# A second buffer for the padded C tile of a Mamba-2 mixer's B/C chains

## The chip, the cores and the metric

The kernel runs on one core of one Trainium2 chip. A core has a matrix engine with its weight loader (PE and PEld in the profile), a vector engine (DVE), a scalar engine for activations and copies (ACT), GpSimd (POOL) and a sync engine (SP) that issues most of the DMAs. The metric is the device time of one execution in microseconds; lower is better.

## The reference

The input x has 4 batches of 256 tokens and 512 channels, all float32. A layer norm gives xn, which feeds two branches:

- a Mamba-2 mixer: `in_proj` gives a gate and x (8192 channels each), B and C (8 groups of 128 channels each) and dt (128 heads). x, B and C pass a causal convolution of 4 taps along the tokens and a silu. Per head, scores C·B with decays multiply x·dt within chunks and between them; the result is gated, normalised by group and projected by `out_proj` to 512 channels.
- a ternary FFN (1792 wide): `silu(x·gate) * (x·up)`, times `down`, then a silu.

The output is `x + mixer * ffn`. What the change touches is the convolution of C:

```python
conv = conv_general_dilated(transpose(xBC, (0, 2, 1)), conv_w, (1,), [(K - 1, 0)],
                            feature_group_count=CONV_DIM, ...)
xBC = silu(transpose(conv + conv_b[None, :, None], (0, 2, 1)))
B = xBC[..., DIN:DIN + G * N].reshape(b, l, G, N)
C = xBC[..., DIN + G * N:].reshape(b, l, G, N)
```

## The kernel before

There are two stages. The first, `front` (L193), lasts until about 302 us; in it the FFN runs on PE while smaller pieces of the mixer are set between its products. The second (from L789) goes over the 64 column tiles of the mixer's x, with the output projection between them.

**The FFN of the front** is a loop of 28 steps (L561): two halves of the tokens by 14 tiles of the FFN's width. A step multiplies by the gate weights (`project_exact`, L289, tile pg), takes a silu on ACT (L566, sg), multiplies by the up weights (L289, pu), combines both on DVE (L575), copies the result on ACT as hh (L583), takes the remainder on DVE as hl (L587), and two steps later multiplies both by the down weights (L297). The integer weights come by DMA on SP (L221) and are cast on POOL (L229).

**The pieces** are called three times in each step (`next(pieces)`); one call is a turn. `all_pieces` (L498) starts a chain `bc_pieces(g)` for group g every 8 turns, from turn 11 on. A new chain is put ahead of the older one, so in a turn that both have, the new one's instructions come first on every queue. Chain g does, a turn to a line:

- turns 0 to 3: four products of two matmul halves each, by Strassen's scheme over B and C at once, in one PSUM bank px; after each, ACT copies the bank into a half of a padded tile (L432): cpad, cpad, then xpad, xpad. cpad holds C and xpad holds B, with three zero columns ahead of each batch of 256 tokens. The next product adds into the same bank, so it waits for the copy.
- turns 4 and 5: three more products (pz and pq); DVE adds them to the halves (L442, L445, L448).
- turn 6: on ACT the last tap of C into cT and of B into bT (L178); on DVE two more taps of C (L182)
- turn 7: the last tap of C and one of B on DVE
- turns 8 and 10: the silus (L187); turns 8 and 9: two more taps of B
- from turn 11: three rounds of scores of C by B on PE (L469, pg); DVE masks two of them (L472) and ACT copies the third (L474) into sc, which SP stores (L476).

Turn 8 of chain g is turn 0 of chain g + 1: the new chain's first copy into cpad stands on ACT's queue ahead of the old chain's silu of C. It writes what the old chain's taps of C read, the last of them issued on DVE in the turn before. In the source the tile cpad, like bT, cT, sc and xpad, has one buffer.

Other pieces share the queues: the sums for the next chain's Strassen weights (L143 to L147, from w, loaded on SP at L134), the dt path, and decay scans of the first ten column tiles (L190, tile em: loaded at L494, stored at L489).

**The order** of the instructions on an engine is that of the source within each stage (`manual_schedule`, L597 and L789). Where the two stages meet, a planner at build time interleaves them on a queue: the load of gm from the second stage (L790) stands among the front's DMAs on SP at 103.9 us, and the first load of a row tile (L622) at 299.3 us.

**PSUM and SBUF.** FFN products, pz, pq and score products take turns in the three banks of `ps_proj`. The tiles of the front's pools (pre, one_of, fp, f2, hp, ep, one behind the other) are laid over again by those of the second stage; a tile there waits for the tiles of the front that lie under it.

Of the kernel before, what the change touches and what calls it, by code (L numbers as in the profile page):

```python
# [43 lines left out]
F32 = mybir.dt.float32  # L44
# [6 lines left out]
P = 128  # L51
NB = 4
# [11 lines left out]
TAPS = 4  # L64
PADW = L + TAPS - 1
# [16 lines left out]
def mixer_ffn(ctx: ExitStack, tc: tile.TileContext, x, in_w, conv_w, conv_b, dt_bias, a_log, d_col,  # L82
              norm_w, out_w, gate_t, up_t, down_t, gate_s, up_s, down_s, out):
    nc = tc.nc
# [46 lines left out]
    def load_w(*tiles):  # L131
        w = wp.tile([P, 2, KT, P], F32, name="w")
        for n, i in enumerate(tiles):
            nc.sync.dma_start(w[:, n], in_w[i])  # L134
        return w

    def blocks(w):
        return [w[:, n, k:k + 2, :] for n in (0, 1) for k in (0, 2)]

    def combine_to(s1, s2, s4, s3, w):  # L140

        a11, a12, a21, a22 = blocks(w)
        nc.vector.tensor_add(s1, a21, a22)  # L143
        nc.vector.tensor_sub(s2, s1, a11)
        yield
        nc.vector.tensor_sub(s4, a12, s2)
        nc.vector.tensor_sub(s3, a11, a21)  # L147
        yield

    def factors(w, s):  # L150
        a11, a12, a21, a22 = blocks(w)
        return a11, a12, a22, s[:, 0], s[:, 1], s[:, 2], a21
# [10 lines left out]
    def halves(xpad):  # L163
        return [xpad[:, 2 * h:2 * h + 2, TAPS - 1:] for h in range(2)]
# [3 lines left out]
    def by_batch(v):  # L168
        return v.rearrange("p (b l) -> p b l", l=L)

    def product(pp, a, b, start, ks=range(KT // 2)):

        for k in ks:
            nc.tensor.matmul(pp, a[:, k, :], b[:, k, :], start=start and k == 0,  # L174
                             stop=k == KT // 2 - 1, skip_group_check=not start)

    def last_tap(i, xT, xpad):
        nc.scalar.mul(xT, xpad[:, :, TAPS - 1:], cw[:, i, TAPS - 1:TAPS])  # L178

    def conv_taps(i, xT, xpad, taps=range(TAPS - 1)):  # L180
        for k in taps:
            nc.vector.scalar_tensor_tensor(xT, xpad[:, :, k:k + L], cw[:, i, k:k + 1], xT,  # L182
                                           ALU.mult, ALU.add)

    def conv_silu(i, xT):
        xf = xT.rearrange("p b l -> p (b l)")
        nc.scalar.activation(xf, xf, AF.Silu, bias=cb[:, i:i + 1])  # L187
# [5 lines left out]
    def front(pre, one_of, fp, f2, hp, ep):  # L193
# [6 lines left out]
        nc.gpsimd.affine_select(out=upto, in_=ones, compare_op=ALU.is_ge, fill=0.0, base=0,  # L200
                                pattern=[[1, P]], channel_multiplier=-1)
        upto_b = upto.unsqueeze(1).to_broadcast([P, NB, P])
        cpad = one_of.tile([P, NB, PADW], F32, name="cpad")
        nc.gpsimd.memset(cpad[:, :, 0:TAPS - 1], 0.0)
        bT, cT = [one_of.tile([P, NB, L], F32, name=n) for n in ("bT", "cT")]
        sc = one_of.tile([P, ROW], F32, name="sc")
        wdt = one_of.tile([P, KT, P], F32, name="wdt")
# [213 lines left out]
        def bc_pieces(g):  # L421


            i_b, i_c = CT + g, CT + G + g
            bpad_h, cpad_h = halves(xpad), halves(cpad)
            a11, a12, a22, s1, s2, s4, s3 = held.pop("a")
            w = load_w(2 * CT + G + g + 1, 2 * CT + g + 1) if g + 1 < G else load_w(0, CT)
            px = ps_t.tile([P, HALF], F32, name="px", tag="t")
            for a, b, to in ((a11, x11, cpad_h[0]), (s2, t2, cpad_h[1]), (s3, t3, bpad_h[1]),
                             (a22, t4, bpad_h[0])):  # L430
                product(px, a, b, a is a11)
                nc.scalar.copy(to, by_batch(px))  # L432
                if a is s2:
                    s = scp.tile([P, 3, KT // 2, P], F32, name="s")
                    held["a"] = factors(w, s)
                    sums = combine_to(s[:, 0], s[:, 1], s[:, 2], blocks(w)[2], w)
                if a is s3 or a is a22:
                    next(sums)
                yield
            pz = ps_proj.tile([P, HALF], F32, name="pz", tag="proj")  # L440
            product(pz, a12, x21, True)
            nc.vector.tensor_add(cpad_h[0], cpad_h[0], by_batch(pz))  # L442
            pq = ps_proj.tile([P, HALF], F32, name="pq", tag="proj")
            product(pq, s1, t1, True)
            nc.vector.tensor_add(bpad_h[1], bpad_h[1], by_batch(pq))  # L445
            yield
            product(pq, s4, x22, False)
            nc.vector.tensor_add(cpad_h[1], cpad_h[1], by_batch(pq))  # L448
            yield
            last_tap(i_c, cT, cpad)  # L450
            last_tap(i_b, bT, xpad)
            conv_taps(i_c, cT, cpad, (0, 1))
            yield
            conv_taps(i_c, cT, cpad, (2,))
            conv_taps(i_b, bT, xpad, (0,))
            yield
            conv_silu(i_c, cT)
            conv_taps(i_b, bT, xpad, (1,))
            yield
            conv_taps(i_b, bT, xpad, (2,))  # L460
            yield
            conv_silu(i_b, bT)
            for _ in range(1 if g + 1 < G else 3):
                yield
            diag = sc[:, 0:T].rearrange("p (b c i) -> p b c i", c=NC, i=P)
            for kb, qb in ((0, 0), (1, 1), (0, 1)):
                pg = ps_proj.tile([P, NB, P], F32, name="pg", tag="proj")
                for b in range(NB):
                    nc.tensor.matmul(pg[:, b, :], bT[:, b, kb * P:(kb + 1) * P],  # L469
                                     cT[:, b, qb * P:(qb + 1) * P], start=True, stop=True)  # L470
                if kb == qb:
                    nc.vector.tensor_tensor(diag[:, :, kb, :], pg, upto_b, ALU.mult)  # L472
                else:
                    nc.scalar.copy(sc[:, T:], pg.rearrange("p b i -> p (b i)"))  # L474
                yield
            nc.sync.dma_start(scores[g], sc)  # L476
# [21 lines left out]
        def all_pieces():  # L498

            turn, chains = 0, [first_pieces()]  # L500
            later = []
            while chains or later or turn < 11 + 8 * G:
                if turn == 6:
                    later.append(dt_pieces())
                if turn >= 11 and (turn - 11) % 8 == 0 and (turn - 11) // 8 < G:
                    chains.insert(0, bc_pieces((turn - 11) // 8))
                if turn == 24:
                    later.append(early_pieces(turn))
                if turn > 11 and (turn - 11) % 8 == 4 and len(chains) > 1:
                    chains.append(chains.pop(0))  # L510
                chains = [c for c in chains if next(c, chains) is None]
                later = [c for c in later if next(c, later) is None]
                turn += 1
                yield
# [82 lines left out]
    with (tc.manual_schedule(), tc.tile_pool(name="pre", bufs=NT) as pre,  # L597
          tc.tile_pool(name="one_of", bufs=1) as one_of, tc.tile_pool(name="fp", bufs=3) as fp,
          tc.tile_pool(name="f2", bufs=2) as f2, tc.tile_pool(name="hp", bufs=1) as hp,
          tc.tile_pool(name="ep", bufs=3) as ep):  # L600
        a, w = front(pre, one_of, fp, f2, hp, ep)
# [187 lines left out]
    with tc.manual_schedule():  # L789
# [4 lines left out]
        for i in range(CT):  # L794
            r, g = i % PER_G, i // PER_G
# [261 lines left out]
        for b in range(NB):  # L1057
            a, f, xb = whole[b]
# [75 lines left out]
```

## Time and profile before

| | us |
|---|---|
| median of three runs | 1728.27 (1727.25 to 1728.54) |
| the profiled execution's own time | 1728.53 |
| its span | 1726.8 |
| the front with the edited chains, about | 43 to 302 |

| engine | busy, us | share of the span |
|---|---|---|
| PE | 1713.8 | 99% |
| PEld | 1107.0 | 64% |
| DVE | 1449.1 | 84% |
| ACT | 1069.9 | 62% |
| POOL | 215.2 | 12% |

In the profile a group of instructions is named by its source line, its engine and `out<-in`, the tiles that it writes and reads. A timeline row gives the start and the duration in us, the engine, the line, the operation, and in brackets the idle time of that engine just before with what ended it. A row of the waits names who waited for whom, the total in us, how often, and the longest. The span is that of the instructions; the execution's own time is 1.73 us longer.

### The profile page before, as it was taken

The page shows a single profiled execution, that of the slowest core. Times are in us where ns is not written, and L with a number is a line of the kernel's source. Part 1 is how long each engine was busy: PE and PEld are TensorE (multiplying, and loading weights), DVE is VectorE, ACT ScalarE, POOL GpSimd, SP SyncE. Part 2 cuts the span into 40 slices and gives each one's busy share as a digit, 9 for nine tenths or more (in the row PEclk, how much of TensorE's full clock was granted, in tenths as well). Part 3 has the DMA queues.
Part 4 walks back from the last instruction along what each step waited for, and adds up shares of the span by engine and source line. Part 5 has one row for each costly group of instructions (what it writes and reads, how often), then busy time and mean ns, then how long its engine had stood idle before and what let it go on. Part 6 is the DMA issues. An engine that isn't in the chain of part 4 may idle for free.

```text
span 1726.8 us, 22575 instructions
## 1 busy us (share of the span) xinstructions
PE 1713.8 (99%) x8494; PEld 1107.0 (64%) x8494; DVE 1449.1 (84%) x1742; ACT 1069.9 (62%) x1428; POOL 215.2 (12%) x238
## 2 busy tenths in 40 slices
PE   8999999999999999999999999999999999999999
PEld 6666667555566666666666666666666666666687
DVE  5768787788888898889888988898889888898876
ACT  4544333688766666666666666666666666666640
POOL 3222323000000000111011100110111011101110
PEclk9999999999999999999999999999999999999999
DMA  6357666576766675777677767776776676767775
GB/s 226 91 168 243 210 230 200 209 222 206 236 198 206 195 216 170 202 201 207 177 206 200 214 188 210 205 216 193 210 203 200 185 210 198 201 172 211 210 229 169
DMA packets 161931, 347.27 MB, mean 201 GB/s; under 512 B 15136, under 2 KB 52896, under 8 KB 161824
## 3 DMA queue, kind: packets, MB, share of 16 engines
q1 hardware_dynamic: 139136, 292.89, 49.4%
q0 software_dynamic: 22688, 52.96, 17.4%
q8 instruction: 67, 1.10, 0.3%
q14 instruction: 40, 0.33, 0.1%
HBM read 236.48 MB, written 81.00 MB: 184 GB/s over the span
## 4 chain that ended last, share of the span: by engine, by line
PE 94%; DVE 3%; DMA 1%; ACT 1%; issue 0%; SPq 0%; ACTq 0%; DVEq 0%
PE px L174 28%; PE po L749 22%; PE pq L174 14%; PE py L693 10%; PE pz L174 7%; PE pp L289 5%; PE tp L649 3%; PE pf L297 2%; PE pg L469 1%; DVE cT L182 1%; PE pv L711 1%; DMA sqacc<-sq 1%; DMA ya<-gated 0%; PE pd L322 0%; DMA wd_i<-in_down_t 0%
## 5 line engine op out<-in xcount | busy, mean ns | idle before, releaser
L174 PE MATMUL px<-xc,w 128*128 128x512 f32 x576 | 271.8, 594 | 0.0
L182 DVE SCALAR_TENSOR_TENSOR xT<-xpad,cw,xT 128x1024 f32<-128x1024 f32 x192 | 246.1, 1282 | 10.0 <-ACT xT L178 5.7
L190 DVE TENSOR_TENSOR_SCAN m<-m,after 128x1024 f32<-128x1024 f32 x108 | 246.5, 2282 | 0.0
L749 PE MATMUL po<-wo,ya 128*128 128x256 f32 x768 | 176.5, 379 | 0.0
L643 DVE TENSOR_TENSOR m<-m,gm 128x1024 f32<-128x1024 f32 x128 | 150.7, 1219 | 14.9 <-ACT m L635 14.9
L693 PE MATMUL py<-m,v 128*64 128x128 f32 x2048 | 160.7, 276 | 0.0
L962 POOL DMA_DIRECT2D sqacc<-sq x54 | 46.1, 853 | 877.4 <-ACT sq L881 812.5
L749 PEld LDWEIGHTS po<-wo,ya 128*128 128x128 f32 x768 | 141.5, 190 | 17.0 <-issue 0.2
L174 PE MATMUL pz<-xnT,w 128*128 128x512 f32 x288 | 145.8, 592 | 0.0
L174 PEld LDWEIGHTS px<-xc,w 128*128 128x128 f32 x576 | 99.4, 190 | 72.2 <-issue 68.9
L174 PE MATMUL px<-xnT,w 128*128 128x512 f32 x288 | 141.8, 615 | 0.0
L174 PE MATMUL px<-xc,s 128*128 128x512 f32 x288 | 135.7, 594 | 2.2 <-ACT cpad L432 2.1
L174 PE MATMUL pq<-xnT,s 128*128 128x512 f32 x288 | 136.2, 595 | 0.2 <-DVE xpad L913 0.2
L174 PE MATMUL pq<-xc,s 128*128 128x512 f32 x288 | 135.3, 592 | 0.0
L635 ACT ACTIVATE m<-m 128x1024 f32<-128x1024 f32 x128 | 134.3, 1058 | 0.6
L649 PEld LDWEIGHTS tp<-ident,xT 128*128 128x128 f32 x512 | 67.8, 141 | 99.5 <-issue 86.4
L693 PEld LDWEIGHTS py<-m,v 128*64 128x64 f32 x2048 | 117.7, 137 | 20.3 <-issue 19.1
L749 PE MATMUL po<-tw,sy 128*128 128x256 f32 x512 | 115.9, 379 | 0.0
L749 PEld LDWEIGHTS po<-tw,sy 128*128 128x128 f32 x512 | 97.2, 190 | 13.2
L855 ACT COPY gT<-px 128x512 f32<-128x512 f32 x64 | 37.5, 586 | 107.8 <-PE px L174 105.0
L693 PE MATMUL py<-mo,v 128*64 128x128 f32 x1024 | 99.7, 273 | 0.0
L174 PEld LDWEIGHTS pq<-xc,s 128*128 128x128 f32 x288 | 54.7, 190 | 68.9 <-issue 62.2
(182 smaller groups left out, 3116.4 us busy)
## 6 DMA issues: line engine op xcount, KB each, us to landing
m<-rows SPq DMA_DIRECT2D x108, 512.0 KB, 6.5
w<-in_in_w SPq DMA_DIRECT2D x144, 256.0 KB, 6.9
mo<-rows SPq DMA_DIRECT2D x128, 256.0 KB, 7.3
gated<-yg SPq DMA_DIRECT2D x64, 512.0 KB, 8.4
ya<-gated SPq DMA_DIRECT2D x30, 1024.0 KB, 7.2
sqacc<-sq POOLq DMA_DIRECT2D x54, 512.0 KB, 6.2
wo<-in_out_w SPq DMA_DIRECT2D x64, 256.0 KB, 6.9
acc<-sa POOLq DMA_DIRECT2D x23, 512.0 KB, 6.0
```

Source lines behind the costliest of these rows:

```text
L174: nc.tensor.matmul(pp, a[:, k, :], b[:, k, :], start=start and k == 0, stop=k == KT // 2 - 1, skip_group_check=not start)
L182: nc.vector.scalar_tensor_tensor(xT, xpad[:, :, k:k + L], cw[:, i, k:k + 1], xT, ALU.mult, ALU.add)
L190: nc.vector.tensor_tensor_scan(m, m, after, 0.0, ALU.add, ALU.mult)
L289: nc.tensor.matmul(pp, w[:, k * P:(k + 1) * P], part[:, k, :], start=(k == 0 and part is xh), stop=(k == KT - 1 and part is xl))
L297: nc.tensor.matmul(pf, part[:, i * P:(i + 1) * P], wd, start=(f == 0 and part is hh), stop=(f == FT - 1 and part is hl))
L635: nc.scalar.activation(m, m, AF.Exp)
L643: nc.vector.tensor_mul(m, m, gm[:, 0:T])
L649: nc.tensor.transpose(tp[:, b, :], xT[:, b, c * P:(c + 1) * P], ident)
L693: nc.tensor.matmul(py[d, q * P:(q + 1) * P], v[:, b, h, :], m, start=False, stop=True, skip_group_check=True)
L749: nc.tensor.matmul(po, a[:, k, :], b[:, k, :], start=start and k == 0, stop=k == HG - 1, skip_group_check=not start)
L855: nc.scalar.copy(gT[:, HALF:], px)
L962: nc.gpsimd.dma_start(sqacc, sq, accum_op=ALU.add)
```

## The change

The single tile cpad becomes two tiles of the same shape, cpad0 and cpad1, each with its zero columns written once by POOL. Chain g uses the one numbered g modulo 2. The rest of the chain, its products, copies, taps and their order, is as before; xpad keeps its one buffer.

```diff
-        cpad = one_of.tile([P, NB, PADW], F32, name="cpad")
-        nc.gpsimd.memset(cpad[:, :, 0:TAPS - 1], 0.0)
+        cpads = [one_of.tile([P, NB, PADW], F32, name=f"cpad{n}") for n in range(2)]
+        for cpad in cpads:
+            nc.gpsimd.memset(cpad[:, :, 0:TAPS - 1], 0.0)
...
             i_b, i_c = CT + g, CT + G + g
+            cpad = cpads[g % 2]
             bpad_h, cpad_h = halves(xpad), halves(cpad)
```

The tile takes 4,144 bytes in each partition.

## The prediction

> **What bounds the kernel now.** I read the page first, for the engine that is never idle.
>
> ```profile
> span 1726.8 us, 22575 instructions
> ...
> PE 1713.8 (99%) x8494; PEld 1107.0 (64%) x8494; DVE 1449.1 (84%) x1742; ACT 1069.9 (62%) x1428; POOL 215.2 (12%) x238
> ...
> PEclk9999999999999999999999999999999999999999
> ```
>
> PE is idle for 13 us in all, and its clock is granted in full. An edit that leaves PE's own work alone can hardly give more than those 13 us. The edited chains run only from 43 to 302 us, so I asked for the busy time of that stage, and then for its waits.
>
> ```profile
> 43.00:302.00 259.00, 256.79 (x1022) 175.83 (x1021) 199.33 (x210) 109.57 (x148) 73.33 (x69) 1.00 0.57 190
> ```
>
> Of 259.00 us PE is busy 256.79, the weight loader 175.83 and DVE 199.33: PE is the bound here too, DVE at 77% is not. The waits (us in total, times, longest):
>
> ```profile
> DVE cpad L448 <- PE pq L174: 18.2, 7, 3.8
> ...
> ACT cpad L432 <- DVE cT L182: 13.1, 5, 4.4
> ...
> PEld px L174 <- ACT cpad L432: 3.9, 4, 1.8
> ```
>
> The second line is the wait the edit removes: ACT's copy of a new chain's product into cpad waits for DVE's taps of the chain before. ACT loses 13.1 us there, but the end of the program is set by PE, and PE loses less: four waits of the weight loader, and it spends about 0.24 us between loads anyway, so 3.9 - 4 x 0.24 = 2.9 us. The PE timeline places them:
>
> ```profile
> 72.59 0.40 PE L297 MATMUL pf<-wd,hl 128*128 128x512 f32 x1
> 73.10 1.98 PE L174 MATMUL px<-xc,s 128*128 128x512 f32 x4
> ...
> 134.08 0.40 PE L289 MATMUL pp<-xl,wg 128*128 128x512 f32 x1
> 135.86 1.98 PE L174 MATMUL px<-xc,s 128*128 128x512 f32 x4 [1.38 <-ACT cpad L432]
> ...
> 165.16 0.40 PE L297 MATMUL pf<-wd,hl 128*128 128x512 f32 x1
> 165.99 1.98 PE L174 MATMUL px<-xc,s 128*128 128x512 f32 x4 [0.44 <-ACT cpad L432]
> ...
> 224.76 0.40 PE L289 MATMUL pp<-xl,wg 128*128 128x512 f32 x1
> 225.41 1.55 PE L174 MATMUL px<-xc,s 128*128 128x512 f32 x3 [0.25 <-ACT cpad L432]
> ```
>
> Neighbouring FFN matmuls start 0.23 us apart, so the products could have started at 72.82, 134.31, 165.39 and 224.99: stalls of 0.28, 1.55, 0.60 and 0.42 us, 2.85 us together, in chains 1, 3, 4 and 6. Chains 2, 5 and 7 pay nothing (chain 7's product starts at 254.95, 0.23 after 254.72).
>
> **The change part by part.**
>
> *Removed: the copy's wait on the taps.* The copy (0.59 us) still needs the first product and whatever stands ahead of it on ACT's queue.
>
> ```profile
> 133.69 0.62 ACT L583 CAST hh<-sg 128x512 fp32r<-128x512 f32 x1 [2.29 <-DVE sg L575]
> 135.22 0.59 ACT L432 COPY cpad<-px 128x512 f32<-128x512 f32 x1 [0.91 <-DVE cT L182]
> 135.70 1.15 ACT L187 ACTIVATE cT<-cT,cb 128x1024 f32<-128x1024 f32 x1
> ```
>
> Chain 1: product done 71.13, copy done by 71.76, ahead of 72.82; the whole 0.28 goes. Chain 4: product done 163.70, copy done 164.33, ahead of 165.39; 0.60 goes. Chain 6: the cast of hh ends 223.72, copy done 224.35, ahead of 224.99; 0.42 goes. Chain 3 differs: the cast ahead of the copy itself waited for DVE until 133.69 and ends 134.31, so the copy ends 134.94 and the product starts 134.99. Of 1.55, 0.87 goes. After a stall the second matmul also comes 0.53 us after the first instead of 0.43 (73.10 to 73.63); 0.10 more goes in chains 1, 4 and 6. Gross: 0.38 + 0.87 + 0.70 + 0.52 = 2.47 us.
>
> *What is late next.* ACT runs straight into L187, which waits for the same third tap; ACT gains only the 0.5 us by which that silu starts earlier. Behind it stand the sigmoid-gate and hh instructions and the next copy. In chain 4, hh waits for DVE until 167.14 and ends 167.75, so the next copy ends 168.38; the product that needs it could start at 169.67 - 0.70 = 168.97, so PE does not see it. Next is the B tile xpad, which keeps one buffer: its copy needs the third B tap, done at 140.38 in chain 3, while its product, done 141.41 before, comes at 140.54. It holds by 0.16.
>
> *Does DVE follow?* Yes, mostly: the first line of the waits says that in seven chains of eight DVE stands idle for PE before L448, 18.2 us in all, so its backlog ends once per chain and an earlier PE starts the next taps earlier. The exception is chain 4:
>
> ```profile
> 171.95 0.42 DVE L143 TENSOR_TENSOR s<-w 128x256 f32<-128x256 f32 x1 [1.32 <-DMA w<-in_in_w]
> 180.51 0.67 DVE L472 TENSOR_TENSOR sc<-pg,upto 128x512 f32<-128x512 f32 x1
> ```
>
> From 171.95 DVE is busy to 181.18, and PE's gate product at 181.63 takes over the bank that L472 empties: 0.45 us of room. That stretch starts with a weight load which SP issued at 164.76 behind a store that waits for a scan on DVE; both move with the gains of chains 1 and 3 (1.25), not with that of chain 4. PE can get ahead of them by 0.45 less 0.05 for the hand-over, 0.40, so 0.30 of chain 4's 0.70 is given back. Net: 2.47 - 0.30 = 2.17 us.
>
> *Added: one memset* (0.11 us, L204). POOL is idle for 3.01 us until 6.72 behind it, waiting for a weight load, so it costs nothing; without that cover, 0.11. The new buffer's own wait is on the chain two back, whose taps ended some 28 us earlier (165.2 against 193.9 for chain 5): nothing.
>
> *Moved: addresses.* One more tile of 4,144 bytes, rounded to 4,160, shifts every later tile of that pool and the four pools behind it; the main pools keep theirs. So the first row tiles of the main loop lie over other tiles: the second now over sc, whose last store is issued at 297.49 and takes 5.2 us at the median. Its load is issued at 308.24, behind two stores that wait for scans, so the store has long landed: nothing. Without that cover, the load would be late by what the store lacks, against room until 323.24, where ACT first reads it. The taps of C and B read different addresses at 1285 and 1280 ns (medians), so I take the address itself as free; bounds 0 and 24 taps by those 5 ns, 0.1 us.
>
> *One rule weighed.* DVE's taps of C last 1274 to 1678 ns, and the one of about 1.6 us at 66.95 lies beside a POOL cast that itself takes 1.67 instead of 0.61. The Trainium skill, Perfetto Trace Analysis, section Optimizing Scalar/DVE Operations, says that GpSimd and DVE share an SBUF read port that a two-port DVE operation locks. By that rule a cast pushed under chain 3's B taps by an earlier PE could cost 0.39 (1678 less 1285 ns), of which xpad's room of 0.16 covers a part, and the saving would be 1.94 instead of 2.17; by the row alone no such push is seen.
>
> **The sum.** Against the profiled execution, 1726.8 of span and 1.73 around it (1728.53), 2.17 less is 1726.36. That run is 0.26 above the median 1728.27, so against the median: 1726.1.
>
> **The rivals.**
>
> *A, all of it goes: 1725.0.* Were chain 3's cast of hh earlier as well and chain 4's bank free, 2.85 + 4 x 0.10 = 3.25 us would go. Against it: the 2.29 us for which that cast waits for DVE, and the row at 180.51. The Trainium skill, Perfetto Trace Analysis, section Optimization Strategy, reads a repeating gap as too few buffers, which would end here with the second one; the rows of chain 3 agree only by half.
>
> *B, the wait moves instead of going: 1727.9.* L187 stands right behind the copy and waits for the same taps, and DVE is 77% busy in this stretch. If DVE and the SP queue did not follow PE, PE could get ahead only by the room at 181.63, 0.40 us. Against it: DVE's idle 18.2 us before L448.
>
> *C, slower: 1728.9.* The SP queue interleaves the two stages when the program is built. The load of gm, from the second stage, stands at 103.95 after a pause of 3.7 us in which SP waits for the store of scores. If the other buffer moved it to right behind that store (96.55), five weight loads would be issued 7.3 us later, the cast of wg would end at 112.6 instead of 105.29, and PE, which reads it at 109.75, would lose 2.8 us: 1726.1 + 2.8. It decides once the gm load is ahead of the wg_i load at 96.99. For it: its place does hang on planned times. Against it: the chain whose scores it loads is the first, which the edit leaves alone.
>
> *D, no effect: 1728.3.* Only if the second tile did not end the wait.
>
> **How the numbers follow.** Forecast 0.62, A 0.11, B 0.14, C 0.06, D 0.02, and 0.05 for a worse order of the queues than C. What a measurement of this kernel can tell from no change is about 0.2%, 3.5 us. A lies at 3.3 us, and about a third of it, with 0.04 of the forecast, passes the bound: faster 0.07. The 0.05, and a little of C: slower 0.06. The rest, 0.87, is no change that counts. The range, 1724.8 to 1729.0, reaches from A to C and leaves out some of A's lower side and the 0.05; the likeliest case alone: 1725.3 to 1727.2, with 0.6 for the spread of runs and the unknowns above.
>
> **What would show it.** No wait of the cpad copy on cT; PE without a gap before the second product in chains 1, 4 and 6, and about 0.7 us in chain 3; PE's idle time from 43 us to the end of the FFN down from 2.2 to below 1; more waiting at L187; the first main-loop product (302.3) about 2 us earlier, and the rest of the trace shifted by as much. It is wrong if the gate product of chain 4 or an xpad copy gains a wait of over a microsecond, if gm or a weight load has another place on SP, or if the shift at 302 is lost by the end.

## The result and the profile after

The changed kernel took 1727.26 us (median of 20 executions) beside 1729.4 for the kernel before on the same chip, a ratio of 0.9986 with a 95% interval of 0.998 to 0.9993. That is 2.1 us; on the earlier median of 1728.27 the ratio gives 1725.85 (1724.8 to 1727.1). The forecast was 1726.1. The interval leaves a saving of 1.2 to 3.5 us: by the times alone no effect (rival D) and B's 0.4 are out, but A's 3.25 is not. What decides between A and the forecast are the rows.

The page of the changed kernel, its span, the busy time of the engines and the row of the granted clock:

```profile
span 1725.4 us, 22572 instructions
...
PE 1715.6 (99%) x8494; PEld 1110.3 (64%) x8494; DVE 1447.5 (84%) x1742; ACT 1069.9 (62%) x1428; POOL 217.9 (13%) x239
...
PEclk9999999999999999999999999999999999999999
```

The span is 1.4 us shorter than 1726.8, and POOL has one instruction more, the memset. The same window of time as before (its length, then busy time and instructions of PE, PEld, DVE, ACT and POOL, the granted clock, the DMA share and GB/s):

```profile
43.00:302.00 259.00, 258.62 (x1030) 177.83 (x1029) 200.79 (x213) 112.75 (x152) 78.11 (x73) 1.00 0.57 194
```

PE was busy for 256.79 of 259.00 us; now it is for 258.62. It is idle for 0.38 instead of 2.21. The waits of the front in the changed kernel (the lines of the file are two further on):

```profile
DVE cpad L450 <- PE pq L174: 18.2, 7, 3.8
...
ACT cpad L434 <- PE px L174: 15.3, 10, 2.8
...
ACT cT L187 <- DVE cT L182: 3.6, 5, 1.4
...
PEld px L174 <- ACT cpad L434: 0.8, 1, 0.8
...
PE px L174 <- ACT cpad L434: 0.4, 1, 0.4
```

There is no wait of ACT's copy on DVE's taps any more; it was 13.1 us. The copy waits for PE's product alone. The weight loader waits for the copy once instead of four times. The silu at L187 waits 3.6 us instead of 1.9. Where the waits stood, the PE timeline shows the last FFN matmul and the second product of chains 1, 3, 4 and 6:

```profile
73.22 0.40 PE L298 MATMUL pf<-wd,hl 128*128 128x512 f32 x1
73.46 1.88 PE L174 MATMUL px<-xc,s 128*128 128x512 f32 x4
...
134.31 0.40 PE L290 MATMUL pp<-xl,wg 128*128 128x512 f32 x1
135.08 1.98 PE L174 MATMUL px<-xc,s 128*128 128x512 f32 x4 [0.38 <-ACT cpad L434]
...
164.38 0.40 PE L298 MATMUL pf<-wd,hl 128*128 128x512 f32 x1
164.61 1.88 PE L174 MATMUL px<-xc,s 128*128 128x512 f32 x4
...
223.25 0.40 PE L290 MATMUL pp<-xl,wg 128*128 128x512 f32 x1
223.48 1.88 PE L174 MATMUL px<-xc,s 128*128 128x512 f32 x4
```

In chains 1, 4 and 6 the product follows by 0.24, 0.23 and 0.23, the pace of the FFN; in chain 3 by 0.77, a stall of 0.55. A group of four products now lasts 1.88 where it lasted 1.98: that is the 0.10 for the restart.

Set side by side by PE's instructions, from the first product of the chains to the first product of the main loop, the stretch fell from 259.67 us (42.47 to 302.14) to 256.49 (43.16 to 299.64). That is 3.18 less, where 2.17 was forecast. It goes by place like this; the last column takes a second profile of the kernel before, from the experiments below:

| place | forecast, us | first profile of before to after | second profile of before to after |
|---|---|---|---|
| chain 1 | 0.38 | 0.40 | 0.40 |
| chain 3 | 0.87 | 1.04 | 1.03 |
| chain 4 | 0.70 less 0.30 | 0.71 | 0.67 |
| chain 6 | 0.52 | 0.55 | 0.13 |
| score products of the last chain (290 to 295) | 0 | 0.44 | about 0.1 |
| the stretch | 2.17 | 3.18 | 2.34 |

The order of SP's and POOL's DMA queues is the same in both kernels.

### The profile page after: what moved, and what is told of

Read it like the earlier page. It is cut to its first block, busy times and chain, and to the rows that moved or that the text cites. A ratio compares the mean times of both kernels' runs of the same rounds, so it can differ in the third digit from the quotient of the medians.

```text
span 1725.4 us, 22572 instructions
## 1 busy us (share of the span) xinstructions
PE 1715.6 (99%) x8494; PEld 1110.3 (64%) x8494; DVE 1447.5 (84%) x1742; ACT 1069.9 (62%) x1428; POOL 217.9 (13%) x239
## 4 chain that ended last, share of the span: by engine, by line
PE 97%; DMA 1%; DVE 1%; ACT 1%; issue 0%; SPq 0%; DVEq 0%; ACTq 0%
PE px L174 29%; PE po L751 22%; PE pq L174 14%; PE py L695 10%; PE pz L174 7%; PE pp L290 5%; PE tp L651 3%; PE pf L298 3%; PE pg L471 1%; PE pv L713 1%; DMA sqacc<-sq 1%; PE pd L323 0%; DMA wd_i<-in_down_t 0%; DMA wdt<-in_in_w 0%; DMA w<-in_in_w 0%
## 5 line engine op out<-in xcount | busy, mean ns | idle before, releaser
L190 DVE TENSOR_TENSOR_SCAN m<-m,after 128x1024 f32<-128x1024 f32 x108 | 246.5, 2282 | 0.0
L943 DVE TENSOR_TENSOR gT<-gT,pq 128x512 f32<-128x512 f32 x63 | 43.2, 686 | 67.3 <-PE pq L174 67.3
```

What stands on the lines that cost most here:

```text
L190: nc.vector.tensor_tensor_scan(m, m, after, 0.0, ALU.add, ALU.mult)
L943: nc.vector.tensor_add(gT[:, HALF:], gT[:, HALF:], pq)
```

## The experiments

"The stretch" is always that from the first product of the chains to the first product of the main loop, in one profiled execution; a stall is the time by which a second product comes later than at the pace of the instructions ahead of it.

**The changed kernel once more.** The first question was whether the profile, 1 us better than forecast, repeats.

> The changed kernel once more, for its granted clock run by run beside that of the kernel before, and to see how far the early part repeats. The stretch from PE's first chain product to its first main-loop product was 259.67 us before and 256.49 in the first profile of the change, 3.2 shorter, while the medians lay 2.1 apart. If the 3.2 is the change, this profile has 256.5 again within 0.2; if it is partly luck of one execution, 256.5 to 257.5. The start up to the first chain product (42.47 before, 43.16 then) and the granted clock are taken for run-to-run scatter: they should differ again, and runs of equal clock should lie about 3 us apart.

Stretch 256.51 us against 256.49, one stall, 0.55 in chain 3. Time 1727.69 us (median of 11) against 1729.8, ratio 0.9985 (0.9976 to 0.9995). The changed kernel's stretch repeats to 0.02 us. At an equal granted clock the two kernels lie 1.4 to 2.2 us apart, not 3 as expected (the last section has the medians).

**Two tiles, one of them used.** What do addresses and the second memset do without the second buffer?

```diff
-            cpad = cpads[g % 2]
+            cpad = cpads[0]
```

> Both tiles and both memsets, so all the moved addresses, but every chain uses the first tile. The theory that the removed wait is all: stalls of 0.28, 1.55, 0.60 and 0.42 us back in chains 1, 3, 4 and 6, a stretch of 259.7 us within 0.3, time as before (0 within 1 us). The rival that the moved addresses give or take something: a stretch off 259.7 by over 0.5 us.

The stalls are back: 0.28, 1.55, 0.26 and 0.35. The stretch is 258.72, not 259.7: 0.95 shorter than that of the kernel before. Time 1729.09 us, ratio 0.9991 (0.9983 to 1.0). So the use of the second tile is worth 2.2 us (258.72 to 256.51), and 0.95 is left that the forecast had no term for. Two runs went after it.

**The kernel before once more, and with a spare tile.** The first is the unchanged kernel; in the second every later tile lies where it lies in the changed kernel:

```diff
         cpad = one_of.tile([P, NB, PADW], F32, name="cpad")
+        one_of.tile([P, NB, PADW], F32, name="spare")
```

> The kernel before, once more, unchanged. From the first product of the chains to the first product of the main loop its profile took 259.67 us; with both tiles of C but only one of them used it took 258.72. If the 0.95 us between them belongs to the kernel (where its tiles lie, or its order), this run gives 259.7 +- 0.1 again; if it is how the casts of POOL happened to fall beside the operations of DVE in one execution, it may give anything from 258.7 to 259.7. The stalls ahead of the second products of chains 1, 3, 4 and 6 are again 0.28, 1.55, 0.3 to 0.6 and 0.35 to 0.42 us. Time against before: same, ratio 1.000 +- 0.001.

> The kernel before with a spare tile of 4,160 bytes a partition, used by nothing, right after the tile of C: every later tile lies where it lies in the changed kernel, and no second memset is issued. If the addresses make the 0.95 us, the stretch takes 258.7 us; if they don't, 259.7 (or what the kernel before shows in its second profile). Stalls ahead of the second products stay at 0.28, 1.55, 0.3 to 0.6 and 0.35 to 0.42. Time against before: 0.9995 if the addresses count, 1.000 if not.

The kernel before again: stretch 258.83, stalls 0.28, 1.55, 0.56 and, in chain 6, 0.02; time 1728.59 us against 1729.49, ratio 0.9997 (0.9988 to 1.0005). With the spare tile: 258.96, stalls 0.28, 1.31, 0.67 and 0.31; time 1729.84, ratio 1.0005 (0.9996 to 1.0014). So the first profile of before was 0.7 to 0.95 longer than three others with the same waits, and the addresses are not needed for it. What differs between two executions of the same kernel is seen at chain 6. The timeline of the kernel before, first profile, the engines mixed:

```profile
222.97 0.61 POOL L229 CAST wg<-wg_i 128x512 fp32r<-128x512 int32 x1 [8.81 <-DMA wg_i<-in_gate_t]
222.98 1.68 DVE L182 SCALAR_TENSOR_TENSOR cT<-cpad,cw,cT 128x1024 f32<-128x1024 f32 x1
...
224.77 0.59 ACT L432 COPY cpad<-px 128x512 f32<-128x512 f32 x1 [1.05 <-DVE cT L182]
```

and in the second profile:

```profile
223.26 1.28 DVE L182 SCALAR_TENSOR_TENSOR cT<-cpad,cw,cT 128x1024 f32<-128x1024 f32 x1
...
223.43 1.59 POOL L229 CAST wg<-wg_i 128x512 fp32r<-128x512 int32 x1 [8.99 <-DMA wg_i<-in_gate_t]
...
224.65 0.59 ACT L432 COPY cpad<-px 128x512 f32<-128x512 f32 x1 [0.65 <-DVE cT L182]
```

In the first, the weight load landed so that POOL's cast started 0.01 us ahead of the third tap of C: the cast took 0.61 and the tap 1.68. In the second the cast started 0.17 behind: the tap took 1.28 and the cast 1.59. The 0.40 is what chain 6 waited for in the first and not in the second. The kernel that uses one of two tiles and the one with the spare tile agree: the cast came first by 0.09 and 0.14, the taps took 1.60 and 1.55, and the stalls of chain 6 were 0.35 and 0.31. At the last chain's scores too, the scan on DVE ahead of them took 2.69 in the first profile, where it began beside a running cast, and 2.28 in the second. The Trainium skill, SBUF — State Buffer, section "SBUF: two separate sides", says that a GpSimd operation that reads SBUF and a DVE operation with two inputs in SBUF lock one pair of ports for a whole instruction, and the one that starts first blocks the other. These rows agree in which one loses; it loses 0.40 of the 0.60 us for which the cast still ran, and 0.98 of the 1.11 for which the tap did, so a little less than the whole. No run moved a cast on purpose, so that this is what makes up the whole 0.7 to 0.95 was read from rows and not tried.

**Chains 3 and 4 alone.** One chain takes the second tile, so that neither it nor the next waits for the chain ahead.

```diff
-            cpad = cpads[g % 2]
+            cpad = cpads[g == 3]
```

> Two tiles, but only chain 3 uses the second; so only the copies of chains 3 and 4 are freed. If each stall belongs to its own copy: 0.28 stays in chain 1 and 0.42 in chain 6, about 0.55 is left in chain 3 and 0 in chain 4; the stretch is 1.00 + 0.70 shorter than 259.67, so 258.0, or 258.3 if 0.3 is given back at the gate product of chain 4 as the prediction has it.

Stretch 257.31; stalls 0.29 (chain 1), 0.55 (3), 0.01 (4), 0.29 (6); one execution took 1727.06 us beside 1731.0. Against the three other profiles with one tile in use (258.72 to 258.96) the two chains are worth 1.4 to 1.65. Chain 4 keeps what it gains, but not because its gate product is free: that starts 0.23 late behind the product ahead, and the matmul after it comes 0.41 later instead of 0.63, which makes up 0.22.

**No decay scans on DVE.** This kernel leaves out the decay scans of the first ten column tiles (L190 on em), so that DVE's queue is shorter; its tables hold the decays unscanned. It asks whether DVE's backlog makes chain 3's taps late.

```diff
-                    decay_scan(m)
```

> The kernel before, one buffer, with the early decay scans left out (20 DVE instructions of 2.3 us in the front; the first ten column tiles then use unscanned rows). If the stall is DVE's backlog ahead of the third tap: chains 3, 4 and 6, which each have a scan right before the taps, lose their stalls (1.55, 0.60, 0.42 to below 0.1), chain 1, which has none, keeps its 0.28; a stretch near 257. If DVE's backlog is not the cause, the stalls stay.

Stretch 258.33. One execution took 1730.26 us beside 1731.0. The stalls of chains 4 and 6 fell to 0.01 and 0.25, chain 1's stayed at 0.28, and chain 3's stayed at 1.53. The timeline of that kernel shows why:

```profile
129.78 1.28 ACT L565 ACT_TABLE_LOAD   x1 [3.03 <-PE pp L289]
131.08 0.69 ACT L565 ACTIVATE sg<-pp,gs 128x512 f32<-128x512 f32 x1
131.66 1.15 ACT L178 ACTIVATE cT<-cpad,cw 128x1024 f32<-128x1024 f32 x1
...
132.84 2.84 DVE L182 SCALAR_TENSOR_TENSOR cT<-cpad,cw,cT 128x1024 f32<-128x1024 f32 x2 [3.67 <-ACT cT L178]
...
136.37 0.62 ACT L582 CAST hh<-sg 128x512 fp32r<-128x512 f32 x1 [2.52 <-DVE sg L574]
```

DVE now stands idle for 3.67 us ahead of chain 3's taps. They are late because ACT, which makes the first tap (L178), waits 3.03 for PE's gate product and then spends 1.28 on loading a table for the silu. In that chain ACT and PE set the time, not DVE's backlog; the expectation that the scans held it was wrong. The kernel before shows the same wait of ACT (3.03) and load of a table (1.28), and DVE idle for 1.48 ahead of these taps although the scan stands there.

**The cast of hh behind the copy.** The forecast held chain 3 to 0.87 by this cast of FFN step 11. Here it is issued after the piece of that turn, so the copy stands ahead of it.

```diff
-            nc.scalar.copy(hh, sg)
+            if n != 11:
+                nc.scalar.copy(hh, sg)
...
             next(pieces, None)
+            if n == 11:
+                nc.scalar.copy(hh, sg)
```

> The changed kernel, with the cast of hh in FFN step 11 issued behind the pieces of that turn, so that chain 3's first copy no longer stands behind it on ACT. If the 0.55 us that PE still stalls in chain 3 is that cast's wait for DVE, the stall goes and the stretch is 0.6 shorter (255.9), time 0.6 less than the change. If it is something else (the bank, the copy's own wait), the stall stays. The late cast could instead hold hl and the down product: then a new wait there, and a stretch as long or longer.

The timeline of that kernel at chain 3:

```profile
131.89 0.59 ACT L434 COPY cpad<-px 128x512 f32<-128x512 f32 x1 [1.25 <-PE px L174]
...
133.31 0.40 PE L290 MATMUL pp<-xl,wg 128*128 128x512 f32 x1
...
133.55 1.88 PE L174 MATMUL px<-xc,s 128*128 128x512 f32 x4
...
134.38 1.15 ACT L187 ACTIVATE cT<-cT,cb 128x1024 f32<-128x1024 f32 x1 [1.90 <-DVE cT L182]
135.44 0.60 ACT L591 CAST hh<-sg 128x512 fp32r<-128x512 f32 x1
```

The copy ends 1.07 us before PE needs it, the stall is gone, and PE is busy in the window for 259.00 of 259.00 us. So the cast's place on ACT's queue was what held chain 3. Stretch 256.13: 0.37 less than 256.5, where 0.6 was expected (0.55 of stall and the restart). The gain at the second product is 0.61, but 0.14 of it is lost at chain 3's third product, whose copy (136.53) now stands behind the moved cast, and 0.13 at chain 4's gate product, which starts 0.46 late, right behind DVE's emptying of its bank; the matmul after it makes up 0.33 of that. This is the place where the forecast had PE held. A PE that is busy for the whole window by these rows is therefore not a PE that nothing holds. Time 1727.75 us, ratio 0.9983 (0.9974 to 0.9992), not told apart from the change alone (0.9985).

**A second tile for B as well.** The forecast named xpad's copy in chain 3 as late next, with 0.16 us of room.

```diff
-            cpad = cpads[g % 2]
-            bpad_h, cpad_h = halves(xpad), halves(cpad)
+            cpad, bpad = cpads[g % 2], (xpad, bpad1)[g % 2]
+            bpad_h, cpad_h = halves(bpad), halves(cpad)
```

(and a tile bpad1, with its zero columns written like the others', and bpad for xpad in the taps of B)

> The changed kernel with a second buffer for the padded tile of B as well. The prediction gave xpad's copy in chain 3 a room of 0.16 us: if so, nothing more to gain, a stretch of 256.5 within 0.2 and the same time as the change. The rival that the wait has moved to B's tile: 0.3 to 1 us less.

Stretch 256.70, the stall of chain 3 at 0.57: no gain, as expected. Its median, 1725.01 us with a ratio of 0.9974 (0.9964 to 0.9983), looks 2 us better all the same. It isn't: 6 of its 9 executions had a mean granted clock of 1.000 (median 1724.80), but 3 of 11 in the run of the changed kernel beside it (median 1724.70).

**B twice and the cast behind, together.**

> The changed kernel with a second padded tile for B too and with the cast of hh of FFN step 11 issued behind the piece of that turn. If the stalls ahead of the second products were all that was left, the stretch takes 256.1 to 256.3 us, no stall stands at the second product of any chain, and the time lies 0.3 to 0.5 us under that of the changed kernel (ratio 0.9974 to 0.9984 against before). If the B tile adds nothing, the result is that of the moved cast alone.

Stretch 256.19, no stall, PE again busy for the whole window; time 1726.63 us against 1729.49, ratio 0.9987 (0.9978 to 0.9996). The stretch is that of the moved cast alone. By the times no version here is shown to beat the changed kernel.

**More work on DVE, with one tile and with two.** One addition of 128x1024 ahead of the third tap of C in each chain, on a tile that nothing else reads (1.4 us each by the rows). This asks what becomes late once the copy no longer waits.

```diff
             yield
+            nc.vector.tensor_add(more, more, more)
             conv_taps(i_c, cT, cpad, (2,))
```

> The kernel before with one more DVE addition (about 1.22 us) ahead of the third tap of C in every chain. If PE waits for that tap by way of the copy, stalls grow by up to 1.22 each: about 1.5, 2.8, 1.8 and 1.6 in chains 1, 3, 4 and 6, 0.5 in chain 7, none in 2 and 5; a stretch about 5.4 us longer than 259.67, so 264 to 265.5. If DVE's time is not what PE waits for: under 1 us longer.

> The changed kernel with the same addition in every chain. If the second buffer has taken the tap out of PE's way, the addition costs little: 0 at the second products apart from the 0.55 of chain 3, and up to 1 us at xpad's copies, which the third B tap, also 1.22 us later, now reaches; a stretch of 256.5 to 258. If the wait had only moved to the silu behind the copy or to the banks, 3 us or more, so over 259.5.

With one tile the stretch takes 268.27, 8.6 more than the first profile of before and 9.4 more than the second, where 5.4 was expected. The stalls of chains 1, 3, 4, 5, 6 and 7 are 1.41, 3.10, 1.78, 0.41, 1.89 and 0.51, together 6.25 more than in the first profile. The clock explains 1.6 of the rest: right behind the stall of 3.10 it was granted at 0.58 from 139 to 142 us, and the matmuls from 138.49 to 143.78 took 5.29 us, where the same ones take 3.68 in the kernel before. One execution took 1736.93 us beside 1731.0. With two tiles it takes 260.25, 3.75 more than the changed kernel's, and 1728.85 us. I expected 0 to 1.5 there. Not one second product is later for it (chain 3's stall stays at 0.55), but the waits of that kernel show other places:

```profile
ACT cT L187 <- DVE cT L182: 12.6, 7, 2.7
...
PEld px L174 <- ACT cpad L436: 3.3, 4, 1.0
...
PEld pg L474 <- ACT bT L187: 1.1, 1, 1.1
```

The silu at L187 waits 12.6 us instead of 3.6, and what stands behind it on ACT's queue waits with it: the copies of the second products, so that PE's third products are late by 0.51 (at 76.91), 0.42 (139.16) and 0.77 (169.62), and in the last chain the silu of B, so that the score product is late by 0.80. The gate product of chain 4 waits 0.98 for its bank, of which the matmul after it makes up 0.32. These are the places that the forecast called late next. They are real; at DVE's own load the change alone hardly reaches them.

## Why the prediction was right, and where it was off

**What bounds the kernel, and the wait that goes.** Right. PE was the bound, its four stalls stood where the timeline put them, and ACT's 13.1 us of waiting was worth only what PE lost of it.

**Chains 1, 4 and 6, gross 0.38, 0.70 and 0.52.** Right in the profile that they were read from: 0.40, 0.71 and 0.55, restart included. For chain 6 the size belonged to the execution: 0.42, 0.02, 0.31 and 0.35 of stall in four profiles with the same waits, and 0.02 in the one where the tap started ahead of the cast. A mean over executions would have had less there. The sign stood in the prediction: its longest tap of C, 1678 ns, is the one at 222.98 that chain 6's copy waits for, but the rule of the Trainium skill was weighed there only for what it might add later.

**Chain 3 held to 0.87.** The mechanism was right: the cast of hh held the copy, and moving the cast took the rest of the stall. The term measured 1.03 to 1.04. The step that was mis-sized is the copy's end behind the cast. I set the durations of cast and copy end to end (0.62, 0.63 and 0.05 to the product), but ACT's rows overlap:

```profile
133.92 0.62 ACT L585 CAST hh<-sg 128x512 fp32r<-128x512 f32 x1 [2.29 <-DVE sg L577]
134.45 0.58 ACT L434 COPY cpad<-px 128x512 f32<-128x512 f32 x1
135.37 1.15 ACT L187 ACTIVATE cT<-cT,cb 128x1024 f32<-128x1024 f32 x1 [0.34 <-DVE cT L182]
```

From the start of the cast to the start of the product at 135.08 it is 1.16 us, not 1.30. That is 0.14 of the 0.16.

**Chain 4 gives back 0.30.** Wrong; this is the step that failed. Nothing was given back, and three things in the term were off.

The first is how far DVE moves. By the forecast the DVE stretch that empties the bank of the gate product would move with chains 1 and 3 only, by 1.25. Counted from the first product of the chains, SP issued the load ahead of that stretch at 120.61 instead of 122.29, 1.68 earlier. The two chains gave 1.44 instead of 1.25, and the scan that the store ahead of the load waits for took 2.46 instead of 2.62. The first operation on the load began 2.08 earlier (127.40 for 129.48), since the load also took 0.4 less, and the emptying of the bank ended 1.91 earlier (136.80 for 138.71), after a scan that took 2.70 instead of 2.28. The gate product came 2.19 earlier, and the room of 0.45 shrank to 0.17.

The second is the hand-over, set at 0.05. Where the gate product waits for this bank (in five of the kernels above), it starts 0.14 to 0.15 behind the end of the emptying. So 0.17 is hardly any room: the place was the right one, and the changed kernel stands at its edge.

The third is what a late start there costs. The rows of the changed kernel, and of the kernel with two tiles of B, where the gate product is held:

```profile
178.82 1.88 PE L174 MATMUL pq<-xc,s 128*128 128x512 f32 x4
180.13 0.79 PE L290 MATMUL pp<-xh,wg 128*128 128x512 f32 x1
180.76 0.40 PE L290 MATMUL pp<-xl,wg 128*128 128x512 f32 x1
```

```profile
178.51 1.88 PE L174 MATMUL pq<-xc,s 128*128 128x512 f32 x4
180.12 0.50 PE L292 MATMUL pp<-xh,wg 128*128 128x512 f32 x1
180.46 0.39 PE L292 MATMUL pp<-xl,wg 128*128 128x512 f32 x1
```

In the second the gate product starts 1.61 behind the group ahead instead of 1.31, so it is 0.30 late, as much as the forecast took off; but the matmul after it follows by 0.34 instead of 0.63, and 0.01 is lost. So even a gate product that is late by 0.30 would have given nothing back. Later starts are not all made up: of 0.46 in the kernel with the moved cast 0.13 is lost.

**What I costed at nothing.** The memset: POOL has one instruction more, and the kernel that has the memset but does not use the tile is at a ratio of 0.9991 (0.9983 to 1.0). The addresses: with the spare tile 1.0005 (0.9996 to 1.0014), and a stretch of 258.96 among 258.72, 258.83 and 259.67 without it or with it. No cost is seen, and none below some 2 us could be by the times; by the stretches the spread between executions, 0.95, hides anything smaller. The queues kept their order, so rival C did not occur. xpad's copy had room: the second tile of B gave nothing, so the price of 0.39 by the rule of the Trainium skill was not paid there. By the rows the rule is borne out at chain 6 of the kernel before, where it decided the size of a stall.

**The sum.** 2.17 forecast; 2.34 between the second profile of before and after, 3.18 from the first, 2.1 by the medians in both comparisons. Of the sum's misses, the 0.30 not given back and the 0.16 of chain 3 raise it to 2.63, and chain 6 at 0.13 instead of 0.52 takes it to 2.24; a tenth at the scores is the rest. That 2.17 came so near is in part luck: two misses of one sign and one of the other cancel, and with the profile that it was worked out from, 1 us is missing. Against all four profiles with one tile in use the change is worth 2.2 to 3.2.

**The rivals.** A (all of it) was right that chain 4 keeps its gain, and wrong on chain 3: its stall went only when the cast was moved. B (the wait moves) had the right places: added DVE work made them bite, and at DVE's real load the gate product of chain 4 took back 0.13 of what the moved cast gained, but nothing of the change alone. D fell with the stalls.

**The shift to the end.** Between the second profile of before and the changed kernel the shift is 2.3 us at the main loop's first product and 3.2 at the end, both taken from the shift of 0.34 with which the chains start: it is kept. Of the 0.9 on top, 0.4 is gained at 468 us, where PE's wait for a transfer is 1.03 instead of 1.47; the other half arose later and was not followed. Between the first profile and the changed kernel 2.5 are gained at 302 us on the page's own clock, but the spans differ by only 1.4. What came in between is a fall of the granted clock at 468 us, told at the end.

## What to carry to other kernels

When a buffer is doubled, take the gain from the engine that sets the end, place by place (2.9 us here), not from the wait that the edit removes (13.1), and look at what else stands ahead of the released instruction on its queue: here one cast held a third of the largest stall, and moving it took that too. Before a late start is counted as lost, see whether the next instruction makes it up: 0.30 late cost 0.01 here. Before a term of half a microsecond is called the kernel's, take a second profile of the same kernel; 0.4 of one stall here was, by the rows, the order in which a transfer happened to land. The places that are late next are worth listing with their room, since added work finds them: one addition per chain cost 9 us with one tile and 4 with two.

## What the runs showed of the hardware

In most executions the mean granted clock was below 1.000. The profiles show that it falls to about half for some 3 us (0.50 from 471 to 474 us in the second profile of the kernel before), after a pause of PE. Windows of the kernel before (first) and of the changed kernel (second), with the clock in the third column from the right:

```profile
466.00:474.00 8.00, 6.61 (x29) 3.84 (x28) 7.17 (x10) 5.63 (x9) 0.00 (x0) 1.00 0.54 187
```

```profile
466.00:474.00 8.00, 8.00 (x31) 4.88 (x32) 5.63 (x10) 4.70 (x6) 0.00 (x0) 0.79 0.25 104
```

In both kernels PE waits for a transfer just before (1.39 and 1.03 us, for sqacc) and then issues 16 products of one column, 1.95 us long. In the first the clock stays at 1.00; in the second it is at 0.79 over the window and at 0.57 from 468 to 472. The shift of PE's instructions against before went from 2.85 us there to 1.19, so the changed kernel's profile lost 1.66 us. The second profile of before lost 1.8 between 471 and 474 (clock 0.72 from 470 to 476) after a pause of 1.47. In the profile of the changed kernel run again the clock was at 0.72 from 24 to 30 us, after a stretch with PE busy for 4.4 of 6 us; in the kernel with one tile and the addition it was at 0.58 from 139 to 142, right behind the stall of 3.10. So the length of the pause alone does not decide it. The Trainium skill, TensorE: Matmul & The Clock Gate, Part 1, tells of a monitor that halves the clock after an idle window of about 3.4 us, and of windows that run freely, wherever the work begins. The runs agree in the size: half the clock for 3.4 us would be an estimated 1.7 us lost, and 1.66, 1.8 and 1.6 were. They agree in that about the same pause costs in one execution and not in another. They do not agree in the idle time: pauses of 1.03 and 1.47 us, each ahead of the products of one column, were enough. Where the windows lay, no trace here shows.

This is most of the spread of the times. By the mean clock of an execution the changed kernel, run again, took 1724.70 us at 1.000 (3 executions), 1727.69 at 0.999 (5) and 1729.47 at 0.998 (3); the kernel before took 1726.85, 1729.48 and 1730.82 (3, 14 and 13). At an equal clock the two differ by 1.4 to 2.2 us, and a step of 0.001 in the clock is worth as much (1.3 to 3.0 us). How many executions stay at 1.000 differs for one kernel too: of the kernel before, 5 in one set of 11 and 1 in another of 27 on the same chip. So a median of few executions carries that count with it.
